# Cross-attention with four key sets: in the first filling slots, SyncE issues the stores of probabilities ahead of refills, weights and half a batch of x

## The chip, the cores and the metric

The kernel runs on one core of one Trainium2 chip. The metric is the device time of one execution in microseconds (us); the time of a kernel is the median of several runs on the same chip. The core has a TensorE (PE, whose weight loads are listed as PEld), a VectorE (DVE), a ScalarE (ACT), a GpSimd (POOL) and a SyncE (SP). Each works through its own instructions in the order in which they were written. SyncE does no arithmetic: it issues nearly all transfers (DMAs) of the main part, and a transfer that has to wait holds up all that are queued behind it.

## The reference

`x` has 32 batches of 512 rows and 640 columns, `ctx` 32 batches of 77 rows and 1024 columns. The reference is an attention of 20 heads of 32 columns. Of its four sets of keys (77 text, 4, 4 and 16 rows) only the first has rows, since the context is 77 rows long; the others add nothing.

```python
q = heads(x @ to_q_w);  k = heads(ctx @ to_k_w);  v = heads(ctx @ to_v_w)
p = softmax(q @ k.T / sqrt(32))
out = merge(p @ v) @ to_out_w + to_out_b + x
```

All matrix products are made in three passes: each float32 operand is split into a high and a low part, and high by high, high by low and low by high are summed.

## The kernel before, in words

A first part (up to about 280 us) projects the context of all batches to keys and values and leaves them in DRAM (`k_dram`, `v_dram`), together with the split output weights (`wo_dram`). The main part is a software pipeline of 160 *slots*, `slot(n)`: slot n belongs to batch b = n // 5 and to the chunk j = n % 5 of 128 columns, that is four heads. The order of instructions is written out by hand. Slots are numbered from 0 here, as in the code.

Of one chunk n of a batch, these steps are made:

- `queries` (L437) makes the queries of chunk n + 1 in slot n, in two parts; `split_q` (L104) splits them into `qt`.
- `scores` (L456, L464) makes the scores of 128 queries at a time: four passes t = 0 to 3 in slot n, on three PSUM buffers, with the maximum taken by VectorE. `exps` (L474) is ScalarE's exponential of a pass.
- In slot n + 1, VectorE takes the reciprocals of the sums, GpSimd normalizes (`normalize`, L489), and VectorE transposes the probabilities into the one buffer `z` (`transpose_p`, L496). SyncE stores `z` to a DRAM tile `pd` in four pieces (L503). The next transposition into `z` has to wait until these four have read it.
- In slot n + 2, `load_p` (L512, L513) loads `pd` back into `raw`, with the keys on the partitions.
- In slot n + 3, `cast_p`, `rest_p` and `last_p` (L523, L529, L530, L537) split `raw` into `pp`; the casts are GpSimd's for the first four chunks and ScalarE's from then on. `values` (L551) multiplies by the value blocks, and `sum_a`, `high_a` and `low_a` (L562 to L576) sum and split the result.
- One batch or two later, `piece` runs the output projection (L594) in slices between the other steps, and `finish` adds the residual and stores (L623, L629).

A slot for which a chunk stands to be split and multiplied, but no output projection yet, is *filling*: these are the slots 3 to 6. From slot 7 on every slot has pieces of the output projection.

Beside these steps, SyncE brings in what later slots need. `refill(b, j, part)` loads in each slot (but j = 4) one group of keys, `kb`, for scores two slots on (L418; at j = 0 of this batch, at j = 2 of the next one), or one group of values, `vb` (L426; at j = 1 and j = 3), in two parts: four key loads in all, or eight value loads. Slots 1, 2 and 3 load the output weights (L706), slot 3 the last fifth. `load_x` (L252) loads quarters of the next batch's x into the one buffer `xs`: for the third batch the first half in slot 4, the second half in slot 5. VectorE transposes that x in place (`transpose_x`, L256) in slots 6 and 7; the first such transposition stands in slot 6 behind the maximum of the second score pass and ahead of that of the third, and every one of them reads all four quarters. `load_residual` (L583) loads rows of x for the residual from slot 6 on.

Transfers that SyncE issues take turns on eight semaphores: one is issued only when the one eight issues ahead of it has landed.

In a filling slot, SyncE's order before was: `load_p`, refill part 0, in slot 5 the two quarters of x, the output weights, refill part 1, from slot 6 on a residual, the four stores of `z`.

Of the kernel before, what the change touches and what calls it, by code (L numbers as in the profile page):

```python
# [8 lines left out]
F32 = mybir.dt.float32  # L9
# [42 lines left out]
def kernel(  # L52
# [25 lines left out]
    nc = tc.nc  # L78
# [4 lines left out]
    NC_ = C // P  # L83
# [16 lines left out]
    wo_dram = dram.tile([P, NC_, 2, C], FPR, name="wo_dram")  # L100
# [144 lines left out]
    def load_x(b, quarters=range(4)):  # L245

        if b not in xss:
            xss[b] = xpool[0].tile([P, S // Q, C // 4], F32, tag="xs", name="xs")
        xs = xss[b]
        src = x[b].rearrange("(a j) (q u) -> q j a u", j=Q, q=4)  # L250
        for q in quarters:
            nc.sync.dma_start(xs[q * Q : (q + 1) * Q, :, :], src[q])  # L252
# [160 lines left out]
    def load_keys(b, g, heads=range(HPC)):  # L413
        j0, nj = GROUPS[g]
        src = k_dram[:, j0 : j0 + nj, :, b * NKEY : (b + 1) * NKEY].bitcast(F32)
        for i in heads:
            r = slice(i * HD, (i + 1) * HD)
            nc.sync.dma_start(kbs[g][r, :, :, i * NKEY : (i + 1) * NKEY].bitcast(F32), src[r])  # L418

    def load_values(b, g, segments=SEGMENTS):  # L420
        j0, nj = GROUPS[g]
        v = v_dram.rearrange("n i j a d -> n j i (a d)")
        for p, t, r0, i, k0, kn in segments:
            k0 += b * NKEY
            c0 = i % 2 * HD
            nc.sync.dma_start(  # L426
                vbs[g][r0 : r0 + kn, :, p, t, c0 : c0 + 3 * HD].bitcast(F32),
                v[k0 : k0 + kn, j0 : j0 + nj, i, :].bitcast(F32),
            )
# [20 lines left out]
    def scores(n, t):  # L450
        b, j = divmod(n, NC_)
        g = GROUP_OF[j]
        qt, kb = qts[n % 2], kbs[g]
        sc = ps.tile([P, S], F32, tag="sc", name="sc", bufs=3)
        for m, (a, c) in enumerate(PAIRS):
            nc.tensor.matmul(  # L456
                sc[:, :KCOLS],
                qt[:, a, t * P : (t + 1) * P],
                kb[:, j - GROUPS[g][0], c],
                start=(m == 0),  # L460
                stop=(m == 2),
            )
        nm = main.tile([P, HPC], F32, tag="nm", name="nm", bufs=3)
        nc.vector.tensor_reduce(  # L464
            nm, sc[:, :KCOLS].rearrange("p (h k) -> p h k", k=NKEY), AX.X, ALU.max, negate=True
        )
        return sc, nm
# [25 lines left out]
    def transpose_p(n):  # L493

        pn = pnb[n % 2]
        nc.vector.transpose(  # L496
            z.rearrange("p b t j -> p t b j"),
            pn.rearrange("p (t h) k -> p t (h k)", t=NQ).rearrange("p t (b i) -> p t b i", i=Q),
        )
        pd = dram.tile([(NBLK + 2) * Q, S], F32, tag="pd", name="pd", bufs=6)  # L500
        rows = pd[: NBLK * Q].rearrange("(b i) q -> i b q", i=Q)
        for a in range(4):
            nc.sync.dma_start(  # L503
                rows[:, :, a * P : (a + 1) * P],
                z[a * Q : (a + 1) * Q].rearrange("p b t j -> p b (t j)"),
            )
        pds[n] = pd
# [11 lines left out]
    def cast_p(n):  # L519

        raw = raws[n]
        pp = late[0].tile([P, 5, S], FPR, tag="pp", name="pp", bufs=1)
        cast(n)(pp[:, 0:2, :], raw[:, 0:2, :])  # L523
        pps[n] = pp

    def rest_p(n):

        raw, pp = raws[n], pps[n]
        cast(n)(pp[:64, 4, :], raw[:64, 2, :])  # L529
        nc.vector.tensor_tensor(  # L530
            pp[:, 2:4, :], raw[:, 0:2, :], pp[:, 0:2, :].bitcast(F32), ALU.subtract
        )
# [33 lines left out]
    def high_a(n):  # L566
        if n >= N - NC_ + 1:
            at = xpool[0].tile([P, 2, S], FPR, tag="xt", name="at", bufs=7)
        else:
            at = late[0].tile([P, 2, S], FPR, tag="at", name="at", bufs=8)  # L570
        nc.scalar.copy(at[:, 0, :], pas[n][:, 0])
        ats[n] = at
# [13 lines left out]
    def add_bias(b, t):  # L586
        nc.gpsimd.tensor_tensor(xrs[b, t], xrs[b, t], bias, ALU.add)  # L587
# [57 lines left out]
    WO = {1: (0, 1, 2), 2: (3,), 3: (4,)}  # L645
    wos = []
# [7 lines left out]
    def refill(b, j, part):  # L654

        heads = range(2 * part, 2 * part + 2)
        segments = SEGMENTS[4 * part : 4 * part + 4]
        if j == 0:
            load_keys(b, 1, heads)
        elif j == 1:  # L660
            load_values(b, 0, segments)
        elif j == 2 and b + 1 < B:
            load_keys(b + 1, 0, heads)
        elif j == 3:
            load_values(b, 1, segments)

    def slot(n, beside=()):
        b, j = divmod(n, NC_)
        ahead, more = n + 1 < N, b + 1 < B
        back, first = PIECES[j]  # L670
        bo_, has_out = b - back, b >= back
        xsplits = SPLIT_X.get(j, ((), ())) if more and n > LATE else ((), ())
        turns = TRANSPOSE_X.get(j, ((), (), ())) if more and b else ((), (), ())
        if b == 1 and j < 2:
            turns = (((), (), ()), ((0, 1), (2,), ()))[j]
        taken = takes.get(n)

        filling = taken is not None and not has_out
        if not filling:
            refill(b, j, 0)  # L680
        if taken is not None:
            cast_p(taken)
        if n - 1 in takes:
            high_a(takes[n - 1])
        s = scores(n, 0)
        if taken is not None:
            rest_p(taken)
        rs = sums(n - 1) if n else None
        if taken is not None:
            last_p(taken)  # L690
        if n:
            normalize(n - 1, rs)
        if n - 1 in takes:
            low_a(takes[n - 1])
        exps(n, 0, *s)
        if ahead:
            queries(n + 1, 0, 2)
        s = scores(n, 1)
        if n - LAG + 1 in pds and n > LATE:
            load_p(n - LAG + 1)  # L700
        if filling:
            refill(b, j, 0)
        if n == NC_:
            load_x(b + 1, (2, 3))
        for k in WO.get(n, ()):
            nc.sync.dma_start(wos[0][:, k].bitcast(F32), wo_dram[:, k].bitcast(F32))  # L706
        refill(b, j, 1)
        finish()
        if j == 4 and b and b + 2 < B:
            load_x(b + 2, (0, 1))  # L710
        if j in RESIDUAL and b >= RESIDUAL[j][0]:
            load_residual(b - RESIDUAL[j][0], RESIDUAL[j][1])
        if j in BIAS and b >= BIAS[j][0]:
            add_bias(b - BIAS[j][0], BIAS[j][1])
        exps(n, 1, *s)
        for i in turns[0]:
            transpose_x(b + 1, i)
        if ahead:
            queries(n + 1, 2, NC_)
        s = scores(n, 2)  # L720
        if not ahead:
            exps(n, 2, *s)
            piece(bo_, first)
            s = scores(n, 3)
        if j == 3 and has_out:
            piece(bo_, first)
            finish()
        if n and has_out:
            transpose_p(n - 1)
        if ahead:  # L730
            split_q(n + 1)
            exps(n, 2, *s)
        if n and not has_out:
            transpose_p(n - 1)
        if j == 4 and b + 2 < B:
            load_x(b + 2, (0, 1) if not b else (2, 3))
        low = nc.vector if filling else nc.gpsimd
        for c in xsplits[0]:
            split_x(b + 1, c, low=low)
        if not ahead:  # L740
            exps(n, 3, *s)
            normalize(n, sums(n))
            finish()
            piece(bo_, first + 1)
            values(taken)
            sum_a(taken)
            return
        if has_out:
            if j != 3:
                piece(bo_, first)  # L750
        else:
            s = scores(n, 3)
        if taken is not None:
            values(taken)
        if len(beside) > 0:
            context_values(LAST, beside[0], psv)
        if has_out:
            s = scores(n, 3)
        finish()
        for i in turns[1]:  # L760
            transpose_x(b + 1, i)
        if taken is not None:
            sum_a(taken)
        for c in xsplits[1]:
            split_x(b + 1, c, low=low)
        exps(n, 3, *s)
        if len(beside) > 1:
            context_values(LAST, beside[1], psv)
        if has_out:
            piece(bo_, first + 1)  # L770
        for i in turns[2]:
            transpose_x(b + 1, i)
# [141 lines left out]
```

## Time and profile before

| | |
|---|---|
| median of 3 runs | 1934.53 us (1933.53 to 1936.31) |
| profiled execution | 1941.03 us, span 1939.2 us |
| busy share of PE, DVE, ACT, POOL | 98%, 74%, 79%, 53% |
| mean granted clock of PE | 0.996 |
| slot 3, 4, 5, 6, 7, 8: first pass of scores ends at about | 297.9, 305.9, 316.1, 327.5, 338.1, 351.0 us of the span |

The profile is of one execution on the chip. Its page lists the engines' busy times, groups of equal instructions and the chain of work that ended last. Its other views are a timeline (start, duration, engine, line, operation, out<-in, and in brackets how long the engine had been idle just before and what ended that), tables of busy time for chosen stretches (the stretch, its length, then for each engine busy time and instructions, the granted clock of PE, the share of the DMA engines' time, GB/s), and for each line of the code the landing of its transfers. `SPq` marks SyncE's queue. Line numbers are those of the kernel before.

### The profile page before, as it was taken

The page shows a single profiled execution, that of the slowest core. Times are in us where ns is not written, and L with a number is a line of the kernel's source. Part 1 is how long each engine was busy: PE and PEld are TensorE (multiplying, and loading weights), DVE is VectorE, ACT ScalarE, POOL GpSimd, SP SyncE. Part 2 cuts the span into 40 slices and gives each one's busy share as a digit, 9 for nine tenths or more (in the row PEclk, how much of TensorE's full clock was granted, in tenths as well). Part 3 has the DMA queues.
Part 4 walks back from the last instruction along what each step waited for, and adds up shares of the span by engine and source line. Part 5 has one row for each costly group of instructions (what it writes and reads, how often), then busy time and mean ns, then how long its engine had stood idle before and what let it go on. Part 6 is the DMA issues. An engine that isn't in the chain of part 4 may idle for free.

```text
span 1939.2 us, 36244 instructions
## 1 busy us (share of the span) xinstructions
PE 1903.6 (98%) x10332; PEld 1699.7 (88%) x10332; DVE 1440.5 (74%) x2337; ACT 1527.0 (79%) x6202; POOL 1019.8 (53%) x673
## 2 busy tenths in 40 slices
PE   9999998999999999999999999999999999999998
PEld 7888886899989989888999998988889988998997
DVE  4444447788788788788888788777788788878875
ACT  3232247898998888888888898889899988888883
POOL 1100056556655665555556555566566655655644
PEclk9999999999999999999999999999999999999999
DMA  9888878888888888988888888988888888888875
GB/s 185 191 198 249 198 192 208 228 238 228 226 225 226 227 227 226 239 231 225 229 234 232 229 228 230 235 232 220 232 236 224 226 228 225 227 229 231 233 210 159
DMA packets 560920, 431.28 MB, mean 222 GB/s; under 512 B 187025, under 2 KB 469073, under 8 KB 560721
## 3 DMA queue, kind: packets, MB, share of 16 engines
q1 hardware_dynamic: 556208, 414.46, 82.7%
q0 software_dynamic: 4416, 14.34, 2.2%
q8 instruction: 84, 1.38, 0.3%
q14 instruction: 116, 0.94, 0.2%
q10 hardware_dynamic: 96, 0.16, 0.0%
HBM read 247.17 MB, written 181.64 MB: 221 GB/s over the span
## 4 chain that ended last, share of the span: by engine, by line
PE 24%; DMA 18%; ACT 18%; issue 13%; DVE 13%; POOL 12%; SPq 3%; DVEq 0%; POOLq 0%; ACTq 0%
ACT pn L474 9%; POOL pn L489 7%; DMA raw<-pd 7%; DMA pd<-z 6%; PE po L594 5%; PE pq L437 5%; PE pv L191 5%; PE pk L191 4%; POOL pp L537 4%; DVE pp L530 3%; ACT xt L263 3%; ACT aw L562 3%; PE sc L456 2%; PE pa L551 2%; DVE nm L464 2%
## 5 line engine op out<-in xcount | busy, mean ns | idle before, releaser
L474 ACT ACTIVATE pn<-sc,nm 128x77 f32<-128x77 f32 x2560 | 800.8, 334 | 76.9 <-DVE nm L464 73.7
L594 PE MATMUL po<-wo_s,at 128*128 128x320 f32 x3840 | 624.5, 310 | 11.2 <-DVE xr L623 7.7
L437 PE MATMUL pq<-xt,wq_s 128*128 128x512 f32 x2400 | 606.5, 393 | 1.2 <-DVE xt L264 1.2
L594 PEld LDWEIGHTS po<-wo_s,at 128*128 128x128 f32 x3840 | 575.3, 188 | 21.5 <-DVE xr L623 17.8
L537 POOL TENSOR_TENSOR pp<-raw,pp 64x512 fp32r<-64x512 f32 x160 | 213.2, 1333 | 631.8 <-ACT pp L529 357.4
L474 ACT ACTIVATION_READ_ACCUMULATOR pn<-sc,nm 128x1 f32 x2560 | 544.5, 213 | 0.0
L437 PEld LDWEIGHTS pq<-xt,wq_s 128*128 128x128 f32 x2400 | 437.0, 188 | 76.8 <-DVE xt L264 1.6
L456 PE MATMUL sc<-kb,qt 128*128 128x308 f32 x1920 | 378.6, 306 | 9.8 <-DMA kb<-k_dram 3.0
L456 PEld LDWEIGHTS sc<-kb,qt 128*128 128x128 f32 x1920 | 324.9, 188 | 56.1 <-ACT pn L474 4.8
L489 POOL TENSOR_TENSOR pn<-pn,rs 128x1232 f32<-128x1232 f32 x160 | 364.1, 2276 | 13.9 <-DVE rs L484 1.6
L496 DVE STREAM_TRANSPOSE z<-pn 128x1280 f32<-128x1280 f32 x160 | 241.8, 1511 | 164.6 <-POOL pn L489 156.1
L464 DVE TENSOR_REDUCE nm<-sc 128x4 f32<-128x308 f32 x640 | 295.2, 462 | 51.6 <-PE sc L456 49.3
L530 DVE TENSOR_TENSOR pp<-raw,pp 128x1024 fp32r<-128x1024 f32 x160 | 196.8, 1230 | 83.5 <-ACT pp L523 72.8
L551 PE MATMUL pa<-pp,vb 128*128 128x512 f32 x960 | 252.6, 398 | 5.1 <-DVE at L576 2.0
L564 DVE TENSOR_TENSOR pa<-pa,aw 64x512 f32<-64x512 f32 x320 | 222.7, 696 | 28.4 <-ACT aw L562 19.0
L264 POOL TENSOR_TENSOR xt<-xs,xt 128x512 fp32r<-128x512 f32 x157 | 200.5, 1296 | 36.1 <-ACT xt L263 35.1
L562 ACT COPY aw<-pa 64x1024 f32<-64x1024 f32 x160 | 161.9, 1012 | 72.8 <-PE pa L551 70.3
L551 PEld LDWEIGHTS pa<-pp,vb 128*128 128x128 f32 x960 | 174.6, 189 | 36.0 <-issue 3.9
L587 POOL TENSOR_TENSOR xr<-xr,bias 128x640 f32<-128x640 f32 x128 | 201.4, 1575 | 0.2
L523 ACT CAST pp<-raw 128x1024 fp32r<-128x1024 f32 x156 | 164.6, 1055 | 35.2 <-DMA raw<-pd 35.2
L191 PE MATMUL pk<-ct,wk_s 128*128 128x512 f32 (+1 forms) x600 | 135.7, 385 | 2.4 <-ACT wk_s L103 1.5
L191 PE MATMUL pv<-ct,wv_s 128*128 128x512 f32 (+1 forms) x600 | 133.7, 381 | 0.0
(46 smaller groups left out, 1345.6 us busy)
## 6 DMA issues: line engine op xcount, KB each, us to landing
pd<-z SPq DMA_DIRECT2D x640, 160.0 KB, 3.9
raw<-pd SPq DMA_DIRECT2D x160, 512.0 KB, 3.9
xs<-in_x_dram SPq DMA_DIRECT2D x128, 320.0 KB, 6.3
xr<-in_x_dram SPq DMA_DIRECT2D x128, 320.0 KB, 4.0
out_dram<-xr SPq DMA_DIRECT2D x127, 320.0 KB, 4.1
raw<-pd SPq DMA_DIRECT2D x160, 128.0 KB, 4.1
v_dram<-vs SPq DMA_DIRECT2D x80, 192.0 KB, 4.0
k_dram<-ks POOLq DMA_DIRECT2D x20, 512.0 KB, 4.2
```

The costliest lines, as they stand in the source:

```text
L191: nc.tensor.matmul(held[j][:, :gn], w[:, k, a, :], cts[g, k][:, c, :gn], start=(k == 0 and n == 0), stop=(k == NK - 1 and n == 2),)
L437: nc.tensor.matmul(pqs[n], wq_s[:, k, a, j * P : (j + 1) * P], xts[b, k][:, c, :], start=(k == 0 and m == 0), stop=(k == NC_ - 1 and m == 2),)
L456: nc.tensor.matmul(sc[:, :KCOLS], qt[:, a, t * P : (t + 1) * P], kb[:, j - GROUPS[g][0], c], start=(m == 0), stop=(m == 2),)
L464: nc.vector.tensor_reduce(nm, sc[:, :KCOLS].rearrange("p (h k) -> p h k", k=NKEY), AX.X, ALU.max, negate=True)
L474: nc.scalar.activation(pnb[n % 2][:, at, :NKEY], sc[:, i * NKEY : (i + 1) * NKEY], AF.Exp, bias=nm[:, i : i + 1], accum_out=sms[n][:, at : ...
L489: nc.gpsimd.tensor_tensor(pf, pf, rs.unsqueeze(2).to_broadcast([P, NQ * HPC, NKEY]), ALU.mult)
L496: nc.vector.transpose(z.rearrange("p b t j -> p t b j"), pn.rearrange("p (t h) k -> p t (h k)", t=NQ).rearrange("p t (b i) -> p t b i", i=Q),)
L530: nc.vector.tensor_tensor(pp[:, 2:4, :], raw[:, 0:2, :], pp[:, 0:2, :].bitcast(F32), ALU.subtract)
L537: nc.gpsimd.tensor_tensor(pp[64:, 4, :], raw[:64, 2, :], pp[:64, 4, :].bitcast(F32), ALU.subtract)
L551: nc.tensor.matmul(pas[n][:, p, :], vb[:, p, t, :], pp[:, c, :], start=(c == p), stop=(t == 1),)
L564: nc.vector.tensor_tensor(pa[64 * p : 64 * p + 64, 0], pa[:64, p], aw[:, p], ALU.add)
L594: nc.tensor.matmul(pos[b, t, h][:, :HALF], ats[b * NC_ + j][:, a, t * P : (t + 1) * P], wos[0][:, j, c, h * HALF : (h + 1) * HALF], start= ...
```

## The change

In the filling slots, the refills, the output weights and the second half of the third batch's x are issued after the stores of `z` instead of ahead of them. In all other slots the order stays as it was. Of the filling slots, slot 4 has no refill (j = 4) and no weights, so its queue is the same.

```diff
+    def weights_and_refill(n):
+        for k in WO.get(n, ()):
+            nc.sync.dma_start(wos[0][:, k].bitcast(F32), wo_dram[:, k].bitcast(F32))
+        refill(*divmod(n, NC_), 1)
...
         s = scores(n, 1)
         if n - LAG + 1 in pds and n > LATE:
             load_p(n - LAG + 1)
-        if filling:
-            refill(b, j, 0)
-        if n == NC_:
-            load_x(b + 1, (2, 3))
-        for k in WO.get(n, ()):
-            nc.sync.dma_start(wos[0][:, k].bitcast(F32), wo_dram[:, k].bitcast(F32))
-        refill(b, j, 1)
+        if not filling:
+            weights_and_refill(n)
         finish()
...
         if n and not has_out:
             transpose_p(n - 1)
+        if filling:
+            refill(b, j, 0)
+            weights_and_refill(n)
+        if n == NC_:
+            load_x(b + 1, (2, 3))
         if j == 4 and b + 2 < B:
             load_x(b + 2, (0, 1) if not b else (2, 3))
```

## The prediction

> **What bounds the kernel now.** I write slots as the code does, from 0; score passes, z, stores and loads carry the number of the slot whose probabilities they hold, so slot 3 transposes and stores the z of 2. The code that the change moves runs in slots 3, 5 and 6 (slot 4 has neither refill nor weights to move). First the table of busy time by stretches: the start of the pipeline against everything behind it, and two stretches in which the granted clock was half.
>
> ```profile
> 303.00:351.00 48.00, 37.32 (x169) 29.10 (x170) 36.02 (x56) 37.10 (x166) 28.18 (x18) 0.96 0.79 193
> 351.00:1900.00 1549.00, 1540.11 (x8658) 1392.57 (x8657) 1246.80 (x2034) 1382.34 (x5779) 919.63 (x576) 1.00 0.86 229
> ...
> 323.70:327.10 3.40, 2.96 (x8) 2.41 (x9) 1.91 (x5) 2.64 (x16) 3.02 (x2) 0.50 0.99 202
> 351.00:354.40 3.40, 3.40 (x10) 2.77 (x10) 2.85 (x5) 3.40 (x13) 0.11 (x2) 0.50 0.80 255
> ```
>
> The third number is PE's busy time. From 351 us on, PE idles 1549.00 - 1540.11 = 8.9 us in all: TensorE is the bound there, and whatever the first slots gain or lose by then is handed to the end one for one. From 303 to 351 us it idles 48.00 - 37.32 = 10.7 us, and the two half-clock stretches of 3.4 us cost up to 1.7 us each. So no more than about 14 us can be won here, and the question is what ends PE's waits. PE's timeline shows the two waits that matter most, with the time idle before each in brackets.
>
> ```profile
> 334.83 1.64 PE L551 MATMUL pa<-pp,vb 128*128 128x512 f32 x6 [1.99 <-DVE at L576]
> ...
> 337.69 0.41 PE L456 MATMUL sc<-kb,qt 128*128 128x308 f32 x1 [0.17 <-DVE qt L104]
> ...
> 348.05 0.44 PE L456 MATMUL sc<-kb,qt 128*128 128x308 f32 x2
> 350.58 0.41 PE L456 MATMUL sc<-kb,qt 128*128 128x308 f32 x1 [2.09 <-DVE qt L104]
> ```
>
> At 337.69 the scores of slot 7 begin in earnest, at 350.58 those of slot 8, after 2.09 us of waiting for VectorE's low half of the queries, qt. VectorE's timeline says why qt is late:
>
> ```profile
> 305.36 1.50 DVE L496 STREAM_TRANSPOSE z<-pn 128x1280 f32<-128x1280 f32 x1
> ...
> 316.74 1.51 DVE L496 STREAM_TRANSPOSE z<-pn 128x1280 f32<-128x1280 f32 x1 [1.06 <-DMA pd<-z]
> ...
> 326.91 1.50 DVE L496 STREAM_TRANSPOSE z<-pn 128x1280 f32<-128x1280 f32 x1
> ...
> 334.99 1.55 DVE L256 STREAM_TRANSPOSE xs<-xs 128x640 f32<-128x640 f32 x2
> ...
> 336.94 0.69 DVE L104 TENSOR_TENSOR qt<-pq,qt 128x512 fp32r<-128x512 f32 x1
> 337.55 1.50 DVE L496 STREAM_TRANSPOSE z<-pn 128x1280 f32<-128x1280 f32 x1
> ...
> 348.44 1.51 DVE L496 STREAM_TRANSPOSE z<-pn 128x1280 f32<-128x1280 f32 x1 [2.78 <-DMA pd<-z]
> ```
>
> There is one z buffer. The transposes of slots 4 (316.74) and 7 (348.44) waited 1.06 and 2.78 us until the stores of the z before had left it. Those stores are issued by SyncE, whose own timeline (start, duration) is the heart of the case:
>
> ```profile
> 305.73 1.98 SPq L426 DMA_DIRECT2D vb<-v_dram  x4
> 307.76 0.43 SPq L706 DMA_DIRECT2D wo_s<-wo_dram  x1
> 308.23 1.88 SPq L426 DMA_DIRECT2D vb<-v_dram  x4
> 310.21 3.38 SPq L503 DMA_DIRECT2D pd<-z  x4
> 316.76 0.38 SPq L512 DMA_DIRECT2D raw<-pd  x1
> ...
> 324.18 0.39 SPq L512 DMA_DIRECT2D raw<-pd  x1
> 324.62 0.47 SPq L513 DMA_DIRECT2D raw<-pd  x1
> 325.14 1.06 SPq L418 DMA_DIRECT2D kb<-k_dram  x2
> 326.25 0.97 SPq L252 DMA_DIRECT2D xs<-in_x_dram  x2
> 327.26 1.95 SPq L418 DMA_DIRECT2D kb<-k_dram  x2
> 331.25 2.23 SPq L503 DMA_DIRECT2D pd<-z  x4
> ...
> 338.02 4.02 SPq L426 DMA_DIRECT2D vb<-v_dram  x8
> ...
> 342.61 3.43 SPq L503 DMA_DIRECT2D pd<-z  x4
> ```
>
> In slot 3 z was ready at 305.36 + 1.50 = 306.9 and its stores began at 310.21; in slot 5, 328.4 and 331.25; in slot 6, 339.1 and 342.61. About 3 us each time, spent behind the refills. GpSimd then waits for the probabilities to come back:
>
> ```profile
> 320.67 1.04 POOL L523 CAST pp<-raw 128x1024 fp32r<-128x1024 f32 x1 [5.16 <-DMA raw<-pd]
> ...
> 344.69 2.28 POOL L489 TENSOR_TENSOR pn<-pn,rs 128x1232 f32<-128x1232 f32 x1
> ```
>
> **The change, part by part.** No instruction is added or removed; three slots reorder SyncE's queue. The landing rows that I use, each minimum, median and maximum from issue to landing: the load of raw at 316.76, the one at 324.18, the second x load at 326.7, all 116 later x loads, all later stores of pd. The last three lines are the four x loads after 366 us, the output weights' load at 307.76 and the load of raw once more, with size and landing.
>
> ```profile
> DMA to landing us min/median/max: 3.8/3.8/3.8
> ...
> DMA to landing us min/median/max: 7.0/7.0/7.0
> ...
> DMA to landing us min/median/max: 8.2/8.2/8.2
> ...
> DMA to landing us min/median/max: 5.0/6.3/7.7
> ...
> DMA to landing us min/median/max: 2.3/3.9/6.5
> ...
> xs<-in_x_dram SPq DMA_DIRECT2D x4, 320.0 KB, 6.7
> ...
> wo_s<-wo_dram SPq DMA_DIRECT2D x1, 640.0 KB, 5.5
> ...
> raw<-pd SPq DMA_DIRECT2D x1, 512.0 KB, 3.8
> ```
>
> *Slot 3.* The four stores begin at 306.9 instead of 310.21 and take 2.2 us (as at 331.25), to 309.1; they have landed by 309.1 + 3.9 = 313.0. The nine moved loads (1.98 + 0.43 + 1.88 = 4.3 us) follow to 313.4, so raw of 2 is issued at 313.4 instead of 316.76, 3.4 us earlier. But it now runs right behind 640 KB of output weights, issued near 311.1 and landing near 316.6. Bounds for its landing: 313.4 + 3.8 = 317.2 with no interference, 313.4 + 7.0 = 320.4 as the load at 324.18, which had 640 KB of x ahead of it. I take 318.9: 316.6 and then 512 KB at the 229 GB/s of the long stretch, 2.3 us. Before it was 316.76 + 3.8 = 320.6, so the gain is 1.7 us (bounds 0.2 and 3.4). The wait of 1.06 us at 316.74 goes too. The moved value blocks land by about 317 and are first read by the values of slot 5, after 324; the cover is 7 us, nothing is lost.
>
> The raw load that is hemmed in by other loads bears on a page of the Trainium skill, "DMA: Bandwidth & Descriptors", section "Queues, rings and completion order": one engine's issues share a ring on each of the DMA engines, and descriptors are consumed in ring order. The trace agrees as far as it goes (3.8 us with nothing fresh ahead, 7.0 us with x ahead); by that rule the early issue is worth 1.7 us, without it 3.4 us, and the rule speaks against the change since it gives the same to the x loads below.
>
> *Slot 5.* GpSimd's cast at 320.67 moves to 319.0, and with it the normalization and the z of 4: 326.91 becomes 325.2, done at 326.7. Its stores then start at 326.7 instead of 331.25. (Before, they started when the raw load at 324.18 had landed, 331.2, eight issues earlier; after, the issue eight back is a store of slot 4, long landed.) Behind them come four key loads (1.06 + about 1.0 us, their waits left out) and then both x loads: 326.7 + 2.2 + 2.1 = 331.0, the second at 331.5. Before, the second was issued at 326.7 and landed 8.2 us later, at 334.9, and **the transposition of that x started at 334.99, so it was just in time**. After, it lands at 331.5 + 6.7 = 338.2; bounds 336.5 (with 5.0) and 339.7 (with 8.2). VectorE works in order: behind this transposition stand the maximum of the third score pass, qt for slot 7 and z. So qt moves from 336.94 to 336.94 + 3.3 = 340.2, PE's score pass from 337.69 to 341.0. PE has nothing else to do there: the values before it end at 336.5 or earlier. The key loads are issued by 331.0 and land well ahead of 341.
>
> *Slot 6.* z is now made at 337.55 + 3.3 = 340.9, done at 342.4, and its stores start at 342.4. Before, they started at 342.61. **What the reorder wins here is already spent by the late x**: the same stores, at the same time. The eight value loads go behind them, 338.02 becomes 344.6, to 348.6, landed by 353; their readers, the values of slot 8, run after 357. The next load of raw follows them, about 1 us later than before; ScalarE, which casts it, then runs late itself.
>
> *Slots 7 and 8.* PE's work from the pass at 337.69 to the end of the passes at 348.05 is 348.49 - 337.69 = 10.8 us, without a wait worth naming. From 341.0 it ends at 351.8. PE was idle for 5 us or so ahead of 341.0; both half-clock stretches of the trace followed stretches with waits of 1.5 to 2.1 us, so I count one such stretch, 1.7 us: 353.5. VectorE: the normalization at 344.69 moves by at most 3.3 to 348.0, done 350.3, then z and qt to 352.4: before 353.5, so the wait of 2.09 us is gone and the half clock behind it as well. Before, the same pass stood at 350.58 with 1.7 us of half clock still to pay: 352.3. **Sum: 353.5 - 352.3 = +1.2 us.**
>
> The clock is also told in the Trainium skill, "TensorE: Matmul & The Clock Gate", section "Part 1: The HAM clock gate (the "warmup" mystery)": after an idle window of about 3.4 us the clock falls to half until a busy window has passed. The two rows at 0.50 agree in length; by that rule the loss of 1.7 us in slot 7 is nearly sure, without it the sum would be -0.5 us.
>
> The sum is against the profiled execution, 1941.03 us (span 1939.2), which becomes 1942.2. The runs' median is 1934.53, 6.5 us lower; I carry the difference over: **1935.7 us**, from about 1933.5 (x at 336.5, or no half clock) to 1937.5 (x at 339.7).
>
> **The rivals.** *The x is in time* (faster). Then slot 6 gives its 3 us: z of slot 7 starts when the normalization ends, 346.97, instead of 348.44, 1.5 us; the gain of up to 1.7 us of slots 3 and 5 may reach it, and the half clock at 351 falls away, 1.7 us. Together -3.2 to -4.9, some -4.3: 1930.2 us. For it speaks that nothing else stands between z and its store. Against it: the x would have to land about 3 us after its issue, and the least of 116 is 5.0.
>
> *The late x costs more than the old wait* (slower). If x lands at 339.7, qt is 4.8 us late, PE arrives at 337.69 + 4.8 + 10.8 + 1.7 = 355.0, +2.7; a second stretch at half clock brings +4.4, 1938.9 us. It decides from the point where x takes about 8 us and PE's idle time spans two stretches of 3.4 us. For it: the x load before took 8.2 us in just this crowd. Against it: the crowd is then ahead of x by some 2 us more.
>
> *It does nothing*: the store's early start is eaten by the next raw load and no x is waited for, since everything has two slots of slack: 1934.5 us. Against it stands the landing at 334.9 beside the start at 334.99.
>
> **How the numbers follow.** Forecast 0.55, does nothing 0.07, x in time 0.13, x costs more 0.25. About 0.2% or 3.9 us is what a measurement of this kernel can tell from no change; within it lie the first two, 0.62; faster 0.13; slower 0.25. The range goes from the faster rival, 1930.0, to a little past the slower one, 1939.5.
>
> **What would show it.** Right: stores of slots 3 and 5 at about 306.9 and 326.7; no wait of z on pd; instead a wait of VectorE on xs of 2 to 5 us at the x transposition in slot 6; PE idle ahead of slot 7's scores, with a row at 0.50 there and none at 351. Wrong: x transposed without a wait (then 1930), or PE still waiting 2 us for qt in slot 8 on top of it (then 1939 and more).

## The result and the profile after

The changed kernel is slower: 1941.4 us median (1939.58 to 1942.79, 6 runs) against 1934.03 us (1932.2 to 1936.31, 6 runs), a ratio of 1.0037 with an interval of 1.0024 to 1.0050. Two further comparisons, on other occasions, gave 1.0020 (1.0011 to 1.0029) and 1.0021 (1.0012 to 1.0031), some 4 us. For scale: the kernel before, compared with itself, gave 0.9990 (0.9981 to 0.9999). Single executions of one kernel spread over some 10 us (33 executions of the kernel before in one comparison: 1934.13 to 1943.04), so one comparison can be off by 0.1 to 0.2%.

The profiled execution took 1941.96 us, hardly more than the one of before (1941.03). Busy time by stretches, as in the prediction, now with the two stretches at half clock that the changed kernel has there:

```profile
303.00:351.00 48.00, 36.19 (x146) 28.73 (x147) 33.31 (x53) 34.65 (x162) 25.33 (x16) 0.86 0.74 182
351.00:1900.00 1549.00, 1539.99 (x8669) 1393.39 (x8668) 1247.49 (x2033) 1383.42 (x5783) 921.17 (x577) 1.00 0.86 229
323.70:330.50 6.80, 6.01 (x15) 4.93 (x16) 5.24 (x10) 5.39 (x26) 4.97 (x5) 0.50 0.69 156
340.80:347.50 6.70, 5.74 (x15) 4.80 (x16) 6.63 (x11) 6.30 (x25) 0.55 (x1) 0.50 0.53 116
```

From 351 us on PE is as busy as before (1539.99 us, before 1540.11). Ahead of it PE made 146 matmuls in the 48 us instead of 169, and the mean granted clock is 0.86 instead of 0.96: two stretches of 6.8 us at half clock instead of one of 3.4. SyncE's timeline (start, duration; line 669 is the weights' load) shows the new order and what it led to:

```profile
307.00 2.72 SPq L503 DMA_DIRECT2D pd<-z  x4
309.76 2.27 SPq L426 DMA_DIRECT2D vb<-v_dram  x4
312.08 0.43 SPq L669 DMA_DIRECT2D wo_s<-wo_dram  x1
312.55 2.81 SPq L426 DMA_DIRECT2D vb<-v_dram  x4
315.46 0.38 SPq L512 DMA_DIRECT2D raw<-pd  x1
...
328.78 2.21 SPq L503 DMA_DIRECT2D pd<-z  x4
331.09 2.52 SPq L418 DMA_DIRECT2D kb<-k_dram  x4
333.65 0.97 SPq L252 DMA_DIRECT2D xs<-in_x_dram  x2
...
335.72 0.58 SPq L583 DMA_DIRECT2D xr<-in_x_dram  x1
343.15 2.21 SPq L503 DMA_DIRECT2D pd<-z  x4
345.46 5.83 SPq L426 DMA_DIRECT2D vb<-v_dram  x8
...
352.33 0.38 SPq L512 DMA_DIRECT2D raw<-pd  x1
```

The stores go out as soon as z is there, at 307.00 and 328.78. The x loads go out at 333.65, before at 326.25. From 336.3 to 343.15 SyncE issues nothing: it stands at the store of slot 6, which has no z yet, and eight value loads and the next load of raw stand behind it. That raw load starts at 352.33, before at 348.40 by the same timeline. VectorE's timeline:

```profile
305.47 1.50 DVE L496 STREAM_TRANSPOSE z<-pn 128x1280 f32<-128x1280 f32 x1
...
315.69 1.50 DVE L496 STREAM_TRANSPOSE z<-pn 128x1280 f32<-128x1280 f32 x1
...
327.25 1.50 DVE L496 STREAM_TRANSPOSE z<-pn 128x1280 f32<-128x1280 f32 x1
...
339.18 1.57 DVE L256 STREAM_TRANSPOSE xs<-xs 128x640 f32<-128x640 f32 x2 [6.01 <-DMA xs<-in_x_dram]
340.67 0.44 DVE L464 TENSOR_REDUCE nm<-sc 128x4 f32<-128x308 f32 x1
341.04 0.67 DVE L104 TENSOR_TENSOR qt<-pq,qt 128x512 fp32r<-128x512 f32 x1
341.63 1.49 DVE L496 STREAM_TRANSPOSE z<-pn 128x1280 f32<-128x1280 f32 x1
...
350.74 1.51 DVE L496 STREAM_TRANSPOSE z<-pn 128x1280 f32<-128x1280 f32 x1 [1.07 <-POOL pn L489]
...
381.88 1.51 DVE L496 STREAM_TRANSPOSE z<-pn 128x1280 f32<-128x1280 f32 x1 [1.97 <-POOL pn L489]
```

The waits of z for the stores (1.06 and 2.78 us before) are gone, at 315.69 and 350.74. In their place stands one of 6.01 us for x, with qt behind it. PE's timeline shows who pays, at the scores of slot 7. Those of slot 8 (354.35) wait for nothing. A short wait follows in slot 10; it is no mark of the loss, since e7, e8 and e13 below, which lose nothing, have it too (1.0 us each).

```profile
341.76 0.63 PE L456 MATMUL sc<-kb,qt 128*128 128x308 f32 x1 [5.72 <-DVE qt L104]
...
354.35 0.59 PE L456 MATMUL sc<-kb,qt 128*128 128x308 f32 x3
...
384.80 1.14 PE L594 MATMUL po<-wo_s,at 128*128 128x320 f32 x6 [0.95 <-DVE xr L623]
```

Since executions differ by several us outside these slots, I compare **the stretch**: the time from the start of the z of chunk 2 (305.36 before, 305.47 after) to that of the z of chunk 9, both in VectorE's timeline. For the kernel before the last one is

```profile
378.31 1.51 DVE L496 STREAM_TRANSPOSE z<-pn 128x1280 f32<-128x1280 f32 x1 [0.78 <-POOL pn L489]
```

so the stretch is 378.31 - 305.36 = 72.95 us before and 381.88 - 305.47 = 76.41 us after. Part of this arises behind the scores of slot 8, where ScalarE, which casts raw in that slot, now waits for it:

```profile
356.14 1.05 ACT L523 CAST pp<-raw 128x1024 fp32r<-128x1024 f32 x1 [0.84 <-DMA raw<-pd]
```

The other two traces of the changed kernel (e5, e12) have 0.65 and 1.47 us there; both traces of the kernel before have no such wait.

### The profile page after: what moved, and what is told of

Read it like the earlier page. It is cut to its first block, busy times and chain, and to the rows that moved or that the text cites. A ratio compares the mean times of both kernels' runs of the same rounds, so it can differ in the third digit from the quotient of the medians.

```text
span 1940.1 us, 36241 instructions
## 1 busy us (share of the span) xinstructions
PE 1903.4 (98%) x10332; PEld 1700.2 (88%) x10332; DVE 1440.3 (74%) x2337; ACT 1527.0 (79%) x6202; POOL 1020.1 (53%) x673
## 4 chain that ended last, share of the span: by engine, by line
PE 28%; ACT 18%; DMA 14%; issue 13%; DVE 12%; POOL 12%; SPq 2%; DVEq 0%; POOLq 0%; ACTq 0%
ACT pn L474 9%; POOL pn L489 8%; PE pq L437 7%; PE po L594 7%; DMA raw<-pd 6%; PE pv L191 5%; PE pk L191 4%; POOL pp L537 4%; DMA pd<-z 4%; PE sc L456 3%; ACT xt L263 3%; DVE pp L530 3%; PE pa L551 3%; ACT aw L562 3%; DVE nm L464 2%
```

## The experiments

Theory A: the loss is the x that lands after VectorE wants it. Rival B: the refills and weights behind the stores hold up the raw loads. All results, with the stretch as above, VectorE's wait ahead of the x transposition of slot 6, and the start of slot 7's raw load, counted from the z of chunk 2 (us; one trace each). Two traces of one kernel differ by up to 1.8 us in the stretch (72.95 and 71.36, 76.19 and 74.43), so a single difference of that size says little by itself.

| kernel | ratio (interval) | stretch | wait for x | raw load |
|---|---|---|---|---|
| before, first profile | - | 72.95 | 0 | 43.0 |
| before again (e1) | 0.9990 (0.9981 to 0.9999) | 71.36 | 0.3 | 41.5 |
| changed, first profile | 1.0037 (1.0024 to 1.0050) | 76.41 | 6.0 | 46.9 |
| changed again (e5) | 1.0020 (1.0011 to 1.0029) | 76.33 | 6.8 | 45.8 |
| changed, third (e12) | 1.0021 (1.0012 to 1.0031) | 75.92 | 6.4 | 46.4 |
| x in its old place (e2) | 0.9989 (0.9980 to 0.9998) | 70.33 | 0 | 40.4 |
| only x moved (e3) | 0.9993 (0.9985 to 1.0002) | 73.32 | 4.1 | 40.7 |
| x transposed later (e4) | 0.9987 (0.9978 to 0.9997) | 71.53 | 1.6 | 40.3 |
| slot 5 only (e6) | 1.0003 (0.9995 to 1.0012) | 74.11 | 4.8 | 41.5 |
| slots 3 and 6 only (e7) | 0.9998 (0.9988 to 1.0008) | 69.53 | 0.2 | 40.2 |
| slots 3 and 5 (e9) | 1.0007 (0.9997 to 1.0016) | 74.74 | 5.7 | 43.5 |
| changed, clock kept (e10) | 1.0005 (0.9997 to 1.0014) | 76.19 | 6.6 | 46.4 |
| the same again (e14) | 1.0011 (1.0002 to 1.0020) | 74.43 | 5.9 | 44.4 |
| slots 3 and 5, clock kept (e13) | 0.9999 (0.9990 to 1.0007) | 74.36 | 6.4 | 42.2 |
| x in old place and transposed later (e8) | 0.9989 (0.9980 to 0.9998) | 69.69 | 0 | 39.4 |
| the same again (e15) | 0.9980 (0.9971 to 0.9990) | 70.80 | 0 | 39.9 |
| slots 3 and 6, x transposed later (e11) | 0.9992 (0.9983 to 1.0001) | 71.18 | 0 | 40.9 |

**The kernel before, once more (e1).** No edit.

> The kernel before, unchanged, run and profiled once more. The question is why its profiled execution (1941.03 us) lay 6.5 us above its runs' median. Theory A (the late x): the profiled execution was a rare one, in which the store of slot 6 and a half clock at 351 us cost what the other executions don't pay; a second profile should then lie near 1934 us, and reach the scores of slot 8 some 4 to 6 us earlier than 350.6, with fewer stretches at half clock. Rival B (the refills): the profile adds a constant 6 us to this kernel, and slot 8 starts at 350 us again. Ratio 1.000 in both.

Measured: the profiled execution took 1939.75 us, again above the median of its runs (1936.81), and the scores of slot 8 came no earlier (350.43 us). So my explanation for the first profile falls: it was no rare execution, and the profile adds no constant 6 us either. Executions of this kernel simply spread from about 1931 to 1943 us.

**The x loads back in their old place (e2).** Ahead of keys and stores, right behind the raw load; the rest as changed:

```diff
+        if n == NC_:
+            load_x(b + 1, (2, 3))
         if not filling:
             weights_and_refill(n)
...
             weights_and_refill(n)
-        if n == NC_:
-            load_x(b + 1, (2, 3))
```

> The changed kernel, with the two x loads of slot 5 back in their old place, right behind the raw load and ahead of keys and stores; refills and weights stay behind the stores. Theory A: the whole loss is the x that lands after VectorE wants it, so this is as fast as the kernel before or faster: 1929 to 1934 us, no wait of VectorE on xs. Rival B: the loss comes from raw loads that now run behind the moved refills and weights; then it stays near 1941 us.

Its VectorE timeline:

```profile
302.16 1.50 DVE L496 STREAM_TRANSPOSE z<-pn 128x1280 f32<-128x1280 f32 x1
...
329.87 0.83 DVE L256 STREAM_TRANSPOSE xs<-xs 128x640 f32<-128x640 f32 x1
...
372.49 1.51 DVE L496 STREAM_TRANSPOSE z<-pn 128x1280 f32<-128x1280 f32 x1 [2.23 <-DMA pd<-z]
```

The x is transposed without a wait, the stretch is 70.33 us, and the time can't be told from that of the kernel before (0.9989, where that kernel against itself gave 0.9990). With refills and weights behind the stores as in the changed kernel, this contradicts B and bears out A.

**Only the x moved (e3).** The kernel before, with `load_x(b + 1, (2, 3))` behind `transpose_p(n - 1)`.

> The kernel before, with nothing changed but the two x loads of slot 5, which go behind the stores of that slot; refills and weights keep their old place. Theory A: 1939 to 1943 us, with VectorE waiting 4 to 7 us for xs in slot 6. Rival B: 1934 us.

The x transposition in VectorE's timeline, and two rows of SyncE's:

```profile
334.17 0.85 DVE L256 STREAM_TRANSPOSE xs<-xs 128x640 f32<-128x640 f32 x1 [4.13 <-DMA xs<-in_x_dram]
```

```profile
330.47 6.44 SPq L426 DMA_DIRECT2D vb<-v_dram  x8
...
338.14 2.61 SPq L503 DMA_DIRECT2D pd<-z  x4
```

The wait is there, 4.13 us, but the time is that of the kernel before: 0.9993, where A said 1939 us or more. **A late x alone costs nothing that can be measured.** SyncE's rows say why: the eight value loads went out at 330.47, while VectorE waited for x, and the store of slot 6 found the queue empty. The late x spends time that the kernel before spent later on, waiting for that store.

**The x transposed later (e4).** The changed kernel, with the three transpositions of slot 6 behind qt, z and the last maximum:

```diff
-            turns = (((), (), ()), ((0, 1), (2,), ()))[j]
+            turns = (((), (), ()), ((), (0, 1, 2), ()))[j]
```

> The changed kernel, with the three transpositions of x of slot 6 moved on VectorE behind the queries' low half, z and the last maximum of that slot; SyncE's order as changed. The x lands as late as before but nothing that TensorE needs stands behind it. Theory A: at least half of the 7 us come back, 1932 to 1937 us, and the stretch at half clock ahead of slot 7 is gone. Rival B: 1940 us or more.

The stretch is 71.53 us, the ratio 0.9987: the whole loss is gone, with SyncE's order as changed. The x still lands late (a wait of 1.57 us is left); what matters is what stands behind its transposition.

**Slot 5 alone, and slots 3 and 6 alone (e6, e7), and the changed kernel again (e5).** In e6 and e7 the new order holds in these slots only.

> The changed kernel, unchanged, run and profiled once more. Theory A (the late x with the half clock behind it) knows of 3.5 to 6 us between the z of chunk 2 and that of chunk 9, and of nothing behind it; so the ratio is 1.002 to 1.003 and the stretch is 75 to 77 us long. Rival C (the seven us of the first comparison were the spread between executions: clock windows that fall at random, waits of up to 1 us on the residual's sum): ratio 0.999 to 1.001. If the ratio is 1.0037 again, a loss behind chunk 9 is missing from A.

> The kernel before, with keys and x behind the stores in slot 5 alone; slots 3 and 6 as before. Theory A: the loss is all here, and more than in the changed kernel, since the early raw load of slot 3 is missing: ratio 1.002 to 1.004, VectorE waiting 4 to 6 us on xs. Rival B (refills of values and weights behind the stores): below 1.001.

> The kernel before, with refills and weights behind the stores in slots 3 and 6; slot 5 as before. Theory A: no loss, 1 to 3 us won between the z of chunk 2 and that of chunk 9 (70 to 71 us), ratio 0.998 to 0.9995. Rival B: 1.002 or more.

The new order of slots 3 and 6 shortens the stretch from 72.95 and 71.36 us to 69.53 when x is in time. When x is late, adding the same two slots to slot 5 lengthens it, from 74.11 to 76.41, 76.33 and 75.92 us. And slot 5 alone stays at 1.0003, below what A expected (1.002 to 1.004). So A lacks a term. VectorE's rows say what is gained, ScalarE's what is paid. In e6 the z of slot 7 no longer waits for the stores (it waits 1.33 us for GpSimd), so the stores of slot 6 have nothing left to win by going first; in the kernel before that wait was 2.78 us. But the raw load of slot 7 now stands behind the moved value loads, and in slot 8 ScalarE waits for it, in e2 and e7 too (0.92 and 1.15 us), and not in e6. (With x transposed later it is gone in e4, e8 and e15.) By these rows, with x in time the gain outweighs this price; with x late only the price is left. (The time of e7, 0.9998, doesn't show the gain of its trace; its interval leaves room for most of it.)

**The value loads ahead again (e9).** Slots 3 and 5 as changed, slot 6 as before.

> The changed kernel with slot 6 as before: the eight value loads ahead of the stores of that slot, so that they don't stand behind a store that waits for z; slots 3 and 5 as changed. Theory A, with a second term (the store of slot 6 waits for z, and z for the late x; the value loads and the next load of raw wait behind it and come 4 to 5 us late): 1 to 2.5 us better than the changed kernel between the z of chunk 2 and that of chunk 9 (74 to 75.4 us), next raw load at 41 to 43 us after the z of chunk 2 instead of 46. Rival D (the late x alone, with its half clock): the same 76.3 us.

```profile
335.71 3.80 SPq L426 DMA_DIRECT2D vb<-v_dram  x4
...
341.10 2.50 SPq L503 DMA_DIRECT2D pd<-z  x4
...
347.18 0.38 SPq L512 DMA_DIRECT2D raw<-pd  x1
```

```profile
352.62 1.05 ACT L523 CAST pp<-raw 128x1024 fp32r<-128x1024 f32 x1
```

The x is nearly as late as before (5.7 us), but the value loads go out while VectorE waits, slot 7's raw load starts at 43.5 us in place of 45.8 to 46.9, and ScalarE's cast (the last row) no longer waits for it. The stretch is 74.74 us, 1.2 to 1.7 us shorter, which alone would be within the scatter of single traces. The times bear it out. On the one occasion on which both ran, the executions of e9 average 1937.94 us and those of the changed kernel (e12) 1940.02, 2.1 us more; e13 and e14 below, which differ by the same edit, average 1935.08 and 1937.48, 2.4 us apart. Each mean is uncertain by some 0.5 to 0.7 us. So about half of the 4 us are **the loads that stand behind a store that waits**. The late x alone (rival D) is not enough.

**The clock kept (e10, e14, e13).** At the end of slot 6, needless matmuls that wait for nothing late; they add work and write into a bank that slot 7 overwrites:

```diff
+        if n == 6:
+            spin = late[1].tile([P, S], F32, tag="po", name="spin", bufs=2)
+            for _ in range(22):
+                nc.tensor.matmul(
+                    spin, wq_s[:, 0, 0, :P], xts[b, 0][:, 0, :], start=True, stop=True
+                )
```

> The changed kernel with 22 needless matmuls of 512 columns (some 4.8 us) on TensorE at the end of slot 6, into a bank that slot 7 overwrites; they add work and need nothing that is late, so they run where TensorE waits 5.7 us for the queries. Theory A (two stretches at half clock, 6.8 us, cost 3.4 of the loss): no row at half clock behind the wait, 2 to 3.4 us better between the z of chunk 2 and that of chunk 9 (73 to 74.5 us), although work was added. Rival E (the wait counts, the half clock is hidden by VectorE and GpSimd, which are late themselves): 76 us or more.

> The changed kernel with the 22 needless matmuls, as in the tenth run, whose trace showed no gain between the z of chunk 2 and that of chunk 9 while its time lay at 1.0005, below the changed kernel's 1.0021. If the half clock costs 3 us: 1.0000 to 1.0010 again. If it costs nothing (rival E): 1.0015 to 1.0028.

> The changed kernel with slot 6 as before (value loads ahead) and the 22 needless matmuls that keep TensorE's clock. If the half clock costs time of its own once the value loads are out of the way: 1 to 2 us better than the value loads ahead alone (1.0007), so 0.9990 to 1.0000. If VectorE and GpSimd hide it (rival E): 1.0007 again, and the passes of slots 7 and 8 wait for the queries as long as before.

Two stretches of e10, and PE's scores of slot 7:

```profile
332.00:340.00 8.00, 5.49 (x25) 4.33 (x24) 2.56 (x5) 1.26 (x7) 1.23 (x1) 1.00 0.87 209
340.00:347.00 7.00, 6.97 (x37) 6.12 (x38) 6.93 (x11) 6.68 (x29) 1.70 (x2) 1.00 0.53 110
```

```profile
340.03 0.41 PE L456 MATMUL sc<-kb,qt 128*128 128x308 f32 x1 [2.53 <-DVE qt L104]
```

The granted clock stays at 1.00, and yet the stretch of e10 is as long as that of the changed kernel, 76.19 us; that of e14, 74.43 us, is shorter, though its trace kept a stretch of 3.4 us at half clock. The two traces don't settle it. The times say more: 1.0005 and 1.0011 against the changed kernel's 1.0020 and 1.0021, and 0.9999 against 1.0007 with the value loads ahead, differences of 0.0008 to 0.0016 or 1.5 to 3 us, each no larger than an interval is wide. On the one occasion on which both ran, the executions of e10 average 1937.80 us and those of e12 1940.02, 2.2 us apart with some 0.5 us of uncertainty each. So the half clock costs time by itself, about 2 us; why e10's stretch doesn't show it stays open. With both edits (e13) the x is as late as ever, 6.4 us, and the time is that of the kernel before, 0.9999 (0.9990 to 1.0007): within that interval these two costs make up the loss, and the late x costs nothing beside them.

**A version that beats the changed kernel, and perhaps both (e8, e15, e11), and the changed kernel a third time (e12).** e8 and e15 are the changed kernel with both edits of e2 and e4; e11 is e7 with the edit of e4.

> The changed kernel with the x loads of slot 5 in their old place and the x transpositions of slot 6 behind the queries and z. Theory A: neither cost is left, so this is the fastest: 68 to 70.5 us between the z of chunk 2 and that of chunk 9, ratio 0.997 to 0.999. Rival B: 1.001 or more.

> The version of the eighth run (x loads in their old place, x transpositions behind the queries, all else as changed), once more, as the candidate that beats both kernels: 0.998 to 0.9995 if its first result holds, 1.000 if it was the spread of the executions.

> The kernel before with refills and weights behind the stores in slots 3 and 6 alone, slot 5 as before, and the x transpositions of slot 6 behind the queries and z. Theory A: it has every gain that was seen and no late x: 68.5 to 70 us between the z of chunk 2 and that of chunk 9, ratio 0.9975 to 0.9995. Rival: the transpositions, later, get in the way of the sum of the values: 71 us or more.

> The changed kernel, unchanged, a third time, since the first two comparisons gave 1.0037 and 1.0020. Theory A (4 us in slots 3 to 10 and nothing else): ratio 1.0015 to 1.0028, 76 to 77 us between the z of chunk 2 and that of chunk 9. If the loss has a part behind that, 1.003 or more.

The version with x in its old place and transposed later took 1933.48 us against 1935.54 and 1932.48 against 1935.73, ratios 0.9989 and 0.9980. Both intervals lie below 1, but so does that of the kernel before against itself (e1, 0.9990), and only e15 goes beyond it: a gain of 0.1 to 0.2% is likely, not shown. e11 is not clear of 1, and its stretch, 71.18 us, is over what was expected. The changed kernel came out at 1.0021, as in the second comparison.

## Why the prediction was wrong

The path to slot 7 was right. The step that failed is the sum of +1.2 us behind it: it had the half clock too small, and it put the late load of raw in slot 7 at nothing. With both the loss is about 4 us. The slower rival names the second stretch at half clock, and its 1938.9 us is close to the later medians, but partly by luck: it has its +4.4 us at the scores of slot 8, where the first trace has +2.3, and it doesn't name the loads that make up the rest. The first comparison's 1941.4 us lies above the range that was given, up to 1939.5; the medians of the two later ones, 1939.59 and 1939.49 us, lie at its edge.

- *The stores of slots 3 and 5 start when z is ready*: right (307.00, forecast 306.9; 328.78, forecast 326.7). The waits of z on pd are gone, as forecast.
- *Slot 3 gains 1.7 us through an earlier raw load*: too much. The nine loads took 5.6 us of SyncE instead of 4.3 (309.76 to 315.4), raw was issued at 315.46, and, in that trace, landed 5.4 us after its issue, with GpSimd waiting for it:

```profile
321.02 1.04 POOL L523 CAST pp<-raw 128x1024 fp32r<-128x1024 f32 x1 [5.41 <-DMA raw<-pd]
```

  Before it was 320.67: no gain. In the other two traces of the changed kernel the z of chunk 4 came 20.56 and 20.83 us after that of chunk 2 (21.78 in the first), before 21.55 and 21.80; the gain is between nothing and 1.2 us. The ring order of the Trainium skill's page "DMA: Bandwidth & Descriptors", section "Queues, rings and completion order", was on the right side of this: the raw load behind 640 KB of weights took 5.4 us (4.3 and 5.5 in the other two traces), that of before, with nothing fresh ahead, 3.8 us.
- *The x lands at 338.2 and VectorE waits for it*: right in kind and nearly in size. It was issued later (334.1 for the second, forecast 331.5) and landed faster, 4.9 us; VectorE started at 339.18, PE at 341.76 (forecast 341.0).
- *One stretch at half clock*: too few. PE was idle for 5.72 us, and the half clock lasted 6.8 us, of which PE worked 5.74 (the row 340.80). From the last scores of slot 7's first pass to the first of slot 8 it took 354.35 - 341.76 = 12.6 us, before 348.05 - 337.69 = 10.4: 2.2 us of cost, forecast 1.7. With the x 0.8 us later than forecast (341.76, not 341.0) this makes the sum +2.3 us at the scores of slot 8 (the last of the pass starts at about 354.6; 352.3 stood against it) instead of +1.2. The second stretch was named as the step that turns the forecast into the slower rival. (Without any half clock the prediction's own rows give +0.1 us, not -0.5, since qt is ready only at 352.4.) The Trainium skill, "TensorE: Matmul & The Clock Gate", section "Part 1: The HAM clock gate (the "warmup" mystery)", has windows of about 3.4 us that run freely; the rows agree, with stretches of 3.4 and 6.8 us. By the experiments PE's clock is about half of the price.
- *The next load of raw follows about 1 us later, and ScalarE "runs late itself"*: this step failed. The prediction did put the store of slot 6 behind the late z (342.4; 343.15 in the trace) and the eight value loads behind the store, but with 4.0 us for these loads; they took 5.8 us of SyncE, and raw came at 352.33, 3.9 us later than before (3 to 5 us by the table). And it put the price of this at nothing, on the ground that ScalarE would be late itself. ScalarE was not that late: it waited 0.84, 0.65 and 1.47 us for the load in the three traces, and GpSimd, VectorE and the z of chunk 7 stand behind its cast. Hence the lag grows again behind slot 8, which the forecast has not: in the first trace from +2.3 us there to 3.5 at the end of the stretch. e9 against e12 and e13 against e14 show its size, 2.1 and 2.4 us.
- *The gain is taken back by the late x, to a net of +1.2 us*: e3 and e6 show this balance at work, 0.9993 and 1.0003. In both the late x and its half clock (6.8 us in both traces) are there, but no raw load that comes late.
- *The profiled execution's distance to the median carries over*: wrong in a different way. 6.5 us was the spread of executions, not a property of the profile. Both profiled executions lay near 1941 us, and their difference of 0.9 us says little; the stretch does. By it the change costs 76.41, 76.33 and 75.92 against 72.95 and 71.36 us, 4.1 us on the mean, which is the 0.2% of the second and third comparison. The further 3 us of the first comparison are in no trace, and their cause stays open; six runs each were few for such a spread.

## What to carry to other kernels

In a queue that issues in order, ask of each moved transfer not only when it lands, but what its consumer's engine has queued behind it: here 640 KB of x held up the queries of the whole next slot, and moving its transposition (e4) was worth as much as moving its load (e2). A store put ahead of loads is a gain only while its data are ready first; as soon as they may be late, the loads wait with it. And where executions spread by 10 us, compare a stretch that the edit touches, between two marks in the trace, rather than two spans.

## What the runs showed of the hardware that I had not expected

Half clock comes in stretches of 3.4 us or twice that, at places that differ between executions of one program: the first profile of the kernel before has none near 265 us, its second one has one of 6.8 us there. Needless matmuls in the wait kept the granted clock at 1.00 there in e10 and e13; in e14 3.4 us at half clock were left. The second x load of slot 5 landed 8.2 us after its issue in the first profile of the kernel before and at most 6.6 us after it in the second; in the first of the changed kernel it was 4.9 us: the landing of one load in one trace is no fixed price.
